# Feature moves in 2048-byte rows, and second-attention statistics one tile per step, in a four-stage gated transformer kernel

## The chip, the cores and the metric

One core of one Trainium2 chip runs the whole program. The metric is device time in microseconds (us) of one execution, less is better. TensorE (PE) multiplies, VectorE (DVE) and ScalarE (ACT) do element-wise work, GpSimd (POOL) does a few small operations, and SyncE (SP) issues most DMAs. Each engine runs its own instructions strictly in the order in which they stand; engines wait for each other by semaphores.

## The reference, cut to what matters

`x` is 8 sequences of 512 tokens with 512 features, in float32. Four stages follow each other, each with a layer norm in front and a gated residual behind.

```python
x = x + tanh(g_xattn[0]) * linear_attention(layernorm(x), ctx, Wq, Wg, bg, Wkv, Wo)   # "xa0"
x = x + tanh(g_ffn[0])   * gelu_ffn(layernorm(x), proj1, proj2)                       # "ff0", 2048 wide
x = x + tanh(g_xattn[1]) * softmax_attention(layernorm(x), ctx, mask)                 # "xa1", 64 context rows
x = x + tanh(g_ffn[1])   * grouped_experts(layernorm(x), router, gate_up, down)       # "ff1", 8 groups of 192
```

The second attention takes scores of the normed x against the 64 context rows, a softmax, and reads the context rows back. The last stage computes eight gated experts for every token (`silu(gate) * up`), weights them by a router that sees the normed x, and sums.

## The kernel before, in words

The batch is cut into 8 blocks of 512 tokens (4 tiles of 128). First the linear attention runs over all blocks, then the first feed-forward over all blocks (`ff0`, block b is called ff0_b), then second attention and experts together (`ff1_b`). Every large product uses a scheme with seven half-size products (m = 1 to 7) in place of eight. One such set of seven is a *unit*. A unit gathers its products in three PSUM banks x, w, z: x takes m = 1, 6, 7, 4 in this order, w takes 5 and 3, z takes 2. After m = 1, 6 and 7 ACT copies the bank x to SBUF (tiles u1, u6, u7, L922), and the next product may be added into that bank only after the copy: m = 6 waits for u1, m = 7 for u6, m = 4 for u7. An ff1 block has six such units in the order 1, 0, 3, 2, 5, 4, and then the down product (`SplitDown`, L1105), whose weights come as tiles of 256 KB from a ring of 16 buffers.

While PE works on one block, a generator (`prep_ff1(b)`) prepares the next one, one step after each product or after several. It has three parts. `normed(..., "xa1_b")` normalizes x for the second attention; `cross_attention` makes the scores (`pst`, L729), turns them (`psc`), takes exponentials (L753), turns back (`pe`), multiplies by the context (`pr`, L774) and adds to x (L776); `normed(..., "ff1_b")` normalizes the new x for the experts; then the router (`plt`, `pl`, `pw`) and the token sums `S` follow. `steps_of` spreads 34 steps over a block.

`normed` is the function that the change touches. DVE takes statistics of the four tiles (`st`, L487; `mv`, L488; `var`, L490; `nshift`, L494), POOL makes 1/sigma (L495, L497), ACT writes the four normed tiles `xn` (L507), DVE transposes them in 32x32 squares (L562), and 16 DMAs from SP's queue (L580), one for each pair of a 32-partition group and a group of feature columns, gather the squares into `xnT`, which has features on partitions. One such DMA moves 64 KB; before the change its rows are 512 bytes: four tiles, 32 partitions each.

Order: some engines run in the order written (`in_order`), the others in an order that a static scheduler works out when the kernel is built. In the last two stages only SP is held to program order, and from ff1 on none; `with here("vector")` holds single DVE instructions to it. The order on each engine is fixed before the run.

## Time and profile before

| what | value |
|---|---|
| median of 3 runs | 2036.1 us (2035.9 to 2041.35) |
| profiled execution, its own time | 2034.87 us |
| its span, first to last instruction | 2033.1 us |
| PE busy | 2003.0 us (99%) |
| DVE busy | 1512.3 us (74%) |
| ACT busy | 646.7 us (32%) |
| SP's DMA queue, share of 16 DMA engines | 73.6% |
| granted TensorE clock, mean | 0.999 |

The time of the profiled execution is what one run took; its span leaves out 1.8 us around it. The names in the trace carry neither block nor unit numbers (`x_ff`, `xnT_xa`), so a block is found by its time: the linear attention ends near 400 us, the ff0 blocks near 1140 us, and an ff1 block takes about 112 us. PE and PEld are the two halves of a product, its stream and its weight load, and two instructions stand for one float32 product.

### The profile page before, as it was taken

To read this page: it belongs to the slowest core of one execution; us is meant where nothing else is said; L and a number is where in the kernel's file an instruction comes from. 1 tells how busy PE (TensorE), PEld (TensorE's weight loads), DVE (VectorE), ACT (ScalarE), POOL (GpSimd) and SP (SyncE) were. 2 spreads that over 40 slices of the span, in tenths; PEclk is the share of its full clock that TensorE was granted. 3 is DMA by queue.
4 is the path that set the end of the run, shared out by engine and by line. 5 is a ranking of instruction groups with operands and counts; after the bars stand their busy time and mean duration, and the time that the engine had idled before them with its cause. 6 is when DMAs were issued, how large, how long until landed. Compare 5 with 4: busy or idle time off the path is not lost.

```text
span 2033.1 us, 34969 instructions
## 1 busy us (share of the span) xinstructions
PE 2003.0 (99%) x12428; PEld 1778.0 (87%) x12428; DVE 1512.3 (74%) x3012; ACT 646.7 (32%) x1294; POOL 95.9 (5%) x147
## 2 busy tenths in 40 slices
PE   9999999999999999999999999999999999999998
PEld 5888887889989899999988989898989888898988
DVE  4788888675857677777857787787778686876858
ACT  4533443323242424233233331313222232313122
POOL 3000000000000000000001010000001010100000
PEclk9999999999999999999999999999999999999999
DMA  7376556688979898989877869787878878786865
GB/s 211 127 217 189 178 156 175 231 304 276 341 236 347 264 341 260 314 291 297 305 245 233 294 217 294 230 291 212 294 238 266 262 234 273 215 288 211 277 203 172
DMA packets 357228, 508.79 MB, mean 250 GB/s; under 512 B 42944, under 2 KB 156768, under 8 KB 352960
## 3 DMA queue, kind: packets, MB, share of 16 engines
q1 hardware_dynamic: 349616, 479.79, 73.6%
q10 hardware_dynamic: 5856, 23.20, 3.1%
q0 software_dynamic: 1584, 3.57, 0.7%
q8 instruction: 100, 1.64, 0.3%
q14 instruction: 72, 0.59, 0.1%
HBM read 413.04 MB, written 69.27 MB: 237 GB/s over the span
## 4 chain that ended last, share of the span: by engine, by line
PE 47%; DVE 1%; DMA 1%; SPq 1%; ACT 0%; issue 0%; POOL 0%; DVEq 0%; POOLq 0%
PE x_ff L910 16%; PE w_ff L910 8%; PE x_ff_down L1105 7%; PE w_ff_down L1105 5%; PE z_ff L910 4%; PE z_ff_down L1105 2%; PE v_ff_down L1105 2%; PE pst L729 1%; PE pr L774 1%; SPq L580 0%; PE plt L789 0%; DMA w_ff<-ff_up 0%; DMA x_ff<-x_ff 0%; DVE xn_ff L562 0%; DVE st_xa L487 0%
## 5 line engine op out<-in xcount | busy, mean ns | idle before, releaser
L910 PE MATMUL w_ff<-S_ff,w_ff 128*128 128x256 f32 x1280 | 305.4, 380 | 2.7 <-DVE up_ff L1003 1.2
L910 PE MATMUL x_ff<-S_ff,w_ff 128*128 128x256 f32 x1280 | 304.0, 379 | 0.0
L910 PE MATMUL x_ff<-xnT_ff,w_ff 128*128 128x256 f32 x1280 | 299.1, 381 | 0.4 <-ACT u_ff L922 0.4
L922 ACT COPY u_ff<-x_ff 128x512 f32<-128x512 f32 x240 | 139.9, 583 | 463.4 <-PE x_ff L910 427.1
L910 PEld LDWEIGHTS w_ff<-S_ff,w_ff 128*128 128x128 f32 x1280 | 240.8, 190 | 39.5 <-DVE up_ff L1003 3.0
L910 PEld LDWEIGHTS x_ff<-S_ff,w_ff 128*128 128x128 f32 x1280 | 242.5, 190 | 34.2 <-ACT a_ff L60 0.8
L910 PEld LDWEIGHTS x_ff<-xnT_ff,w_ff 128*128 128x128 f32 x1280 | 240.4, 191 | 34.2 <-issue 1.8
L1105 PE MATMUL x_ff_down<-w_ff_down,split_ff_down 128*128 128x128 f32 x1344 | 161.8, 275 | 0.0
L1105 PEld LDWEIGHTS x_ff_down<-w_ff_down,split_ff_down 128*128 128x128 f32 x1344 | 155.8, 192 | 0.0
L910 PE MATMUL z_ff<-xnT_ff,w_ff 128*128 128x256 f32 x640 | 152.8, 380 | 0.0
L1119 DVE TENSOR_TENSOR part_ff_down<-part_ff_down 128x128 f32<-128x128 f32 x315 | 83.9, 285 | 73.2 <-ACT part_ff_down L1132 64.2
L910 PEld LDWEIGHTS z_ff<-xnT_ff,w_ff 128*128 128x128 f32 x640 | 119.9, 190 | 19.9 <-issue 4.5
L1105 PE MATMUL w_ff_down<-w_ff_down,split_ff_down 128*128 128x128 f32 x896 | 107.9, 275 | 0.0
L1105 PEld LDWEIGHTS w_ff_down<-w_ff_down,split_ff_down 128*128 128x128 f32 x896 | 103.9, 192 | 0.0
L970 ACT ACTIVATE a_ff<-a_ff,b_sb 128x256 f32<-128x256 f32 x128 | 58.1, 501 | 91.9 <-DVE a_ff L965 91.9
L1105 PE MATMUL w_ff_down<-w_ff_down,s_ff 128*128 128x128 f32 x672 | 83.1, 275 | 2.6 <-ACT part_ff_down L1132 2.6
L965 DVE TENSOR_TENSOR a_ff<-w_ff,u_ff 128x512 f32<-128x512 f32 x64 | 43.9, 685 | 53.8 <-ACT u_ff L922 53.2
L1105 PEld LDWEIGHTS w_ff_down<-w_ff_down,s_ff 128*128 128x128 f32 x672 | 80.1, 192 | 3.6 <-ACT part_ff_down L1132 2.8
L1003 DVE TENSOR_TENSOR up_ff<-w_ff,u_ff 128x512 f32<-128x512 f32 x96 | 65.6, 683 | 23.6 <-ACT u_ff L922 23.3
L1105 PE MATMUL x_ff_down<-w_ff_down,a_ff 128*128 128x128 f32 x672 | 82.8, 275 | 0.0
L1105 PEld LDWEIGHTS x_ff_down<-w_ff_down,a_ff 128*128 128x128 f32 x672 | 79.5, 192 | 0.4
L993 DVE SCALAR_TENSOR_TENSOR g_ff<-th_ff,x_ff 128x512 f32<-128x512 f32 x48 | 32.6, 680 | 63.2 <-ACT th_ff L992 63.2
(262 smaller groups left out, 3266.7 us busy)
## 6 DMA issues: line engine op xcount, KB each, us to landing
w_ff_down<-stream_ff SPq DMA_DIRECT2D x680, 256.0 KB
w_ff<-ff_up SPq DMA_DIRECT2D x560, 256.0 KB
stream_ff<-build_ff_down SPq DMA_DIRECT2D x49, 448.0 KB
x_ff<-x_ff SPq DMA_DIRECT2D x16, 1024.0 KB
share<-shares SPq DMA_DIRECT2D x64, 256.0 KB
xnT_ff<-xn_ff SPq DMA_DIRECT2D x240, 64.0 KB
ff_up<-build_ff_up SPq DMA_DIRECT2D x42, 256.0 KB
x_ff<-x_xa ACTq DMA_DIRECT2D x8, 1024.0 KB
```

The costliest lines, as they stand in the source:

```text
L729: nc.tensor.matmul(pst[ts(r, M), :], lhsT=ctxT[:, c, :], rhs=features_of("ff1", xnT)[:, c].rearrange("p (u r q) i -> p r u q i", u=2, r=2) ...
L774: nc.tensor.matmul(pr[t], lhsT=eT[half, t // 2, :], rhs=c2[half, :], start=True, stop=True)
L910: nc.tensor.matmul(p[:, n, :], lhsT=w[:, c, ts(n, P)], rhs=moving, **self.mark(m, 2 * n + c),)
L922: nc.scalar.copy(self.s[m], p)
L965: nc.vector.tensor_tensor(h, p, s, ALU.add)
L970: nc.scalar.activation(h[:, n, :], p[:, n, :], AF.Gelu, bias=b1_sb[:, f : f + 1])
L993: nc.vector.scalar_tensor_tensor(g, th, 1.0, p, ALU.add, ALU.mult)
L1003: nc.vector.tensor_tensor(u, p, s, ALU.add)
L1105: nc.tensor.matmul(p[bank][:, place, :], lhsT=operand[k][:, c, :], rhs=w[at // 4][:, ts(at % 4, P)], start=bank not in opened, stop=True, ...
L1119: return lambda: nc.vector.tensor_tensor(m(k), m(k), m(by), ALU.add)
```

## The change

Two parts, both in `normed`.

The tiles `xn` and `xnT` get another order of their free dimensions. `xn` was [tile, column group, 128], and is [column group, tile, 128]; `xnT` was [tile, q, 128], and is [q, tile, 128]. So the 16 gathering DMAs move 32 rows of 2048 bytes each in place of 128 rows of 512 bytes. All readers of `xnT` (token sums, `Up.product`, `pst`, `plt`) address it in the new order; `S` is laid out as (q, tile, column) outside the first attention.

The statistics of `xa1_b` keep DVE's program order, one tile per generator step (three more `yield`s). What comes behind them in `prep_ff1` so moves three steps back; `steps_of` stays 34.

```diff
-        xnT = work.tile([P, NC, S] if ph == "xa0" else [P, NT, NC, P], F32, tag="xnT", name=f"xnT_{tag}")
+        xnT = work.tile([P, NC, S] if ph == "xa0" else [P, NC, NT, P], F32, tag="xnT", name=f"xnT_{tag}")
...
-        with here(*(["vector"] if held or ph == "xa0" else [])):
+        with here(*(["vector"] if held or ph == "xa0" or tag.startswith("xa1") else [])):
             for t in range(NT):
                 st = small.tile([P, 6], F32, tag="st", name=f"st_{tag}_{t}")
                 nc.vector.bn_stats(st, xb[:, t, :])
                 nc.vector.bn_aggr(mv[:, t, :], st)
+                if tag.startswith("xa1") and t < NT - 1:
+                    in_order.discard("vector")
+                    yield
+                    in_order.add("vector")
...
-        xn = bank["xn"].tile([P, NT, D], F32, tag="xn", name=f"xn_{tag}")
+        xn = bank["xn"].tile([P, NC, NT, P], F32, tag="xn", name=f"xn_{tag}")
...
-                nc.vector.transpose(xn[:, at[t], :], xn[:, at[t], :])
+                nc.vector.transpose(xn[:, :, at[t], :], xn[:, :, at[t], :])
...
-                    nc.sync.dma_start(out=xnT[ts(l, HD), :, q, :], in_=xn[ts(q, HD), :, ts(l, P)])
+                    nc.sync.dma_start(out=xnT[ts(l, HD), q], in_=xn[ts(q, HD), l])
...
-        return xnT.rearrange("p t q (c i) -> p c (t q) i", c=NC)
+        return xnT.rearrange("p q t (c i) -> p c t q i", c=NC)
...
+            a11, a12, a21, a22 = (xnT[:, :, ts(r, 2), ts(h, 2 * HD)] for r in range(2) for h in range(2))
+            to = s.rearrange("p k c (q t i) -> p k (c q) t i", q=2, t=2)
...
-                        1: v[:, c, 0:8],
+                        1: v[:, c, 0:2],
```

The built programs have the same number of matmuls and of SP's DMAs in each kernel. Up to the last ff0 block (ff0_7) the two PE orders are the same; from there on the scheduler places the prepared work differently. In the ff1 blocks 1 to 6 of the changed kernel, for example, PE runs `pr`, then one matmul of m = 2 of the fourth unit (unit 2), then m = 6, 5, 7 of that unit, m = 1 of the next, and m = 4; ACT runs u6, th1, two of the four `xn` norms of `ff1_b`, u7, the other two norms.

More of the change, by code (lines that the diff above doesn't have):

```diff
@@ L528, in turn @@
                     nc.scalar.copy(
-                        xnT[:, t].rearrange("p q (c i) -> p c q i", c=NC),
+                        xnT[:, :, t].rearrange("p q (c i) -> p c q i", c=NC),
                         pt.rearrange("p c (q i) -> p c q i", q=NC),
@@ L568, in normed @@
                     t,
-                    xn[:, at[t], :].rearrange("p (l c e) -> p c l e", l=NC, c=NC),
+                    xn[:, :, at[t]].rearrange("p l (c e) -> p c l e", c=NC),
                     lambda of: of.rearrange("p (c l e) -> p c l e", l=NC, c=NC),
@@ L589, in features_of @@
         if ph == "xa0":
-            return xnT.rearrange("p c (g i) -> p c g i", i=HD)
-        return xnT.rearrange("p t q (c i) -> p c (t q) i", c=NC)
+            return xnT.rearrange("p c (t q i) -> p c t q i", q=NC, i=HD)
+        return xnT.rearrange("p q t (c i) -> p c t q i", c=NC)
     turned = [dram.tile([P, NC, M], F32, tag=f"turned{b}", name=f"turned_{b}") for b in range(B)]
@@ L681, in token_combinations @@
         s = work.tile([P, 4, 2, H2], F32, tag="S", name=f"S_{ph}_{b}", bufs=1)
-        v = features_of(ph, xnT)
-        a11, a12 = v[:, 0:2, 0:8], v[:, 2:4, 0:8]
-        a21, a22 = v[:, 0:2, 8:16], v[:, 2:4, 8:16]
-        to = s.rearrange("p k c (g i) -> p k c g i", i=HD)
+        if ph == "xa0":
+            v = features_of(ph, xnT).rearrange("p c t q i -> p c t (q i)")
+            a11, a12, a21, a22 = (v[:, ts(h, 2), ts(r, 2)] for r in range(2) for h in range(2))
+            to = s.rearrange("p k c (t i) -> p k c t i", t=2)
+        else:
+            a11, a12, a21, a22 = (xnT[:, :, ts(r, 2), ts(h, 2 * HD)] for r in range(2) for h in range(2))
+            to = s.rearrange("p k c (q t i) -> p k (c q) t i", q=2, t=2)
         nc.vector.tensor_tensor(to[:, 0], a21, a22, ALU.add)
@@ L689, in token_combinations @@
         nc.vector.tensor_tensor(to[:, 3], a12, to[:, 1], ALU.subtract)
-        return s
+        if ph == "xa0":
+            return to.rearrange("p k c t (q i) -> p k c t q i", i=HD)
+        return to.rearrange("p k q t (c i) -> p k c t q i", c=2)
     def prep_ff0(b):
@@ L731, in cross_attention @@
                     lhsT=ctxT[:, c, :],
-                    rhs=features_of("ff1", xnT)[:, c].rearrange("p (u r q) i -> p r u q i", u=2, r=2)[:, r],
+                    rhs=features_of("ff1", xnT)[:, c].rearrange("p (u r) q i -> p r u q i", r=2)[:, r],
                     start=c == 0,
@@ L791, in prep_ff1 @@
                     lhsT=router_sb[:, c, :],
-                    rhs=features_of("ff1", xnT)[:, c, ts(t, NC)],
+                    rhs=features_of("ff1", xnT)[:, c, t],
                     start=c == 0,
@@ L901, in product @@
                     moving = {
-                        1: v[:, c, 0:8],
-                        2: v[:, 2 + c, 0:8],
-                        4: v[:, 2 + c, 8:16],
-                        5: s[:, 0, c, :],
-                        6: s[:, 1, c, :],
-                        7: s[:, 2, c, :],
-                        3: s[:, 3, c, :],
+                        1: v[:, c, 0:2],
+                        2: v[:, 2 + c, 0:2],
+                        4: v[:, 2 + c, 2:4],
+                        5: s[:, 0, c],
+                        6: s[:, 1, c],
+                        7: s[:, 2, c],
+                        3: s[:, 3, c],
                     }[m]
```

## The prediction

> **What bounds the kernel now.** I read the page first: PE is busy 99% of the span, so a change is worth what it takes from, or adds to, PE's waits. Then the windows of 50 us, to see where PE waits; then the timeline there, for what each wait ends on; then PE's order in the two built programs.

> ```profile
> PE 2003.0 (99%) x12428; PEld 1778.0 (87%) x12428; DVE 1512.3 (74%) x3012; ACT 646.7 (32%) x1294; POOL 95.9 (5%) x147
> ...
> 1000.00:1050.00 50.00, 47.36 (x336) 44.74 (x335) 35.16 (x84) 14.72 (x29) 1.54 (x2) 1.00 0.85 279
> 1050.00:1100.00 50.00, 43.94 (x256) 35.41 (x255) 29.96 (x76) 24.19 (x53) 5.60 (x9) 0.97 0.71 228
> ...
> 1300.00:1350.00 50.00, 50.00 (x349) 45.84 (x348) 42.51 (x92) 14.06 (x29) 5.61 (x9) 1.00 0.82 264
> ```

> The first number after the stretch is its length, the next PE's busy time. The ff0 and ff1 blocks run without a wait, except where the first ff1 block is prepared (1000 to 1100). There:

> ```profile
> 1009.06 2.93 ACT L507 ACTIVATE xn_xa<-x_ff,nshift_xa,rstd_xa 128x512 f32<-128x512 f32 x4 [6.22 <-POOL nshift_xa L497]
> 1012.51 1.16 PE L1105 MATMUL w_ff_down<-w_ff_down,s_ff 128*128 128x128 f32 x8 [2.64 <-ACT part_ff_down L1132]
> 1062.20 1.99 PE L774 MATMUL pr<-ctxd,eT 64*128 64x512 f32 x8
> 1066.86 1.99 PE L910 MATMUL w_ff<-S_ff,w_ff 128*128 128x256 f32 x8 [1.18 <-DVE x_ff L776]
> 1070.84 2.93 ACT L507 ACTIVATE xn_ff<-x_ff,nshift_ff,rstd_ff 128x512 f32<-128x512 f32 x4 [0.87 <-POOL nshift_ff L497]
> 1074.54 11.56 SPq L60 DMA_DIRECT2D xnT_ff<-xn_ff  x16
> 1092.77 0.99 PE L1105 MATMUL v_ff_down<-w_ff_down,a_ff 128*128 128x128 f32 x6 [3.01 <-DMA w_ff_down<-stream_ff]
> 1093.55 3.54 PE L910 MATMUL x_ff<-xnT_ff,w_ff 128*128 128x256 f32 x8
> ```

> Four norms hold ACT for 2.93 us, PSUM copies stand behind them, PE waits 2.64 us. Later 16 moves hold SP for 11.56 us, weight tiles stand behind them, PE waits 3.01 us, and the next eight matmuls take 3.54 us where 1.89 is usual: the clock was halved.

> **What the change takes away.** *Moves.* One took 599 ns to issue (median), a weight tile, also in rows of 2048 bytes but with 128 of them, 320:

> ```profile
> L60 SPq DMA_DIRECT2D xnT_ff<-xn_ff x128: 585/599/1986, 408.7 to 1085.5; - x128
> L1493 SPq DMA_DIRECT2D w_ff_down<-stream_ff x296: 319/320/1732, 1188.8 to 2013.0; - x148
> ```

> The new move has 32 rows; between a quarter of 599 and 599 I take 320, so a batch takes 16 x 0.32 = 5.1 us, not 9.6 to 11.6. [...] I take the rows, but only the first block's batch is on PE's path. SP's new order also puts the two tiles for v_ff_down and the 1 MB x load ahead of it. Behind the batch stands tile 9: issued near pr + 17.5, needed near pr + 26.

> *First block.* In ACT's new order the norms of xa1_0 stand behind those copies (2.64 gone); their new place is ahead of u7 of ff0_7's first unit, due 11.7 us after the old block's last down product. Six small sums, two gated additions, two statistics and the copies before them put nshift at 5.9, the norms at 7.2 to 10.1, u7 at 10.7: 1.0 to spare, and a wait at that place if DVE is later than that. The accumulator lent to pr is next opened 6.9 us after pr, not 3.5, past DVE's 4.6 (1.18 gone). With the batch, the waits for plt (0.78), pl (0.38) and v_ff_down (3.01), the half clock (3.54 - 1.89 = 1.65) and 0.40 before pw go: 6.2. Together **10.0 us**.

> *Second block.* At 1188.61 and 1191.84 PE waits 0.43 and 1.24 for ACT and DVE, after DVE stood 2.79 us before a statistic whose x had not landed; program order places it later: **1.7**. Two waits for plt in later blocks: **1.2**. Sum **12.9 us**.

> **What costs nothing.** Transposes, norms and S take strided operands, as they do now: same element counts, 0.70, 0.73 and 0.68 us. Matmuls read runs of 32 elements from xnT already, 1.73 us for eight, as S contiguous. Were a strided matmul 1% slower, the page's 4480 of L910 in ff units at 0.216 us (1.73 / 8) would cost 10; nothing in the rows says so. POOL's xa1 pair moves behind the router products and three DMA issues; POOL is 5% busy. The xa1 moves go behind three to seven weight loads and x stores or shares; pst has slack of 8 us there. Shares go some eight tiles later, still a block's down product ahead.

> **What it adds.** Three steps later means other neighbours on ACT. Row, in the block at 1390:

> ```profile
> 1390.90 1.99 PE L774 MATMUL pr<-ctxd,eT 64*128 64x512 f32 x8
> ...
> 1393.42 0.74 DVE L776 SCALAR_TENSOR_TENSOR x_ff<-pr,coef,x_ff 128x512 f32<-128x512 f32 x1
> ...
> 1401.92 0.69 DVE L487 BATCH_NORM_STATS2 st_xa<-x_ff 128x6 f32<-128x512 f32 x1
> ...
> 1402.59 0.16 DVE L494 TENSOR_SCALAR nshift_ff<-mv_ff 128x4 f32<-128x4 f32 x1
> ...
> 1404.11 0.81 ACT L507 ACTIVATE xn_ff<-x_ff,nshift_ff,rstd_ff 128x512 f32<-128x512 f32 x1 [3.50 <-POOL nshift_ff L497]
> ```

> From pr to the first norm 13.21 us. Before, only u1 of a later unit stood behind it, with 1.3 us to spare (done 1405.4, wanted 1406.7). After, u7 of unit 2 stands behind two norms, and m = 4 waits for u7. In the new DVE order the first addition to x isn't late (pr + 1.16, as at 1063.36, not 2.52), two sums (1.20) and a st_xa (0.61) leave the stretch: 13.21 - 3.17 = 10.0. Two norms 1.43, u7 0.59: pr + 12.1. PE reaches m = 4 at 1.92 (pr) + 0.43 + 4 x 1.73 = 9.25. **A wait of 2.85 us**, in each of the six preparations of blocks 2 to 7. Low end: the first block's 8.64 (1062.20 to 1070.84), a wait of 1.4; high end: 13.21, a wait of 6.0. I take the row of the same kind of block less what left it.

> Two smaller ones, per block. At the start, three statistics (3 x 0.70) now stand ahead of DVE's up at 1373.00; the four xa1 norms then end near 1382.1, u6 of the second unit at 1382.65, wanted at 1382.25: 0.4 (0 to 2.5, if DVE is later). Between psc and pe 3.5 us are planned, th2 ahead of the exponentials makes it 3.7: 0.2 (0 to 1). Sum 6 x 3.45 = **20.7**.

> Preparing block 1, three norms stand before u7: 8.64 + three DVE operations 1.8 + 2.14 + 0.59 = 13.2 against 11.0: **2.2**. Block 0: four norms before u6 of the last ff0 unit, 8.64 + 2.86 + 0.59 = 12.1 against 10.6: 1.5, and 0.3 at pe: **1.8**.

> The new waits are near 3 us, so the clock must be asked. [...] Rows: a gap of 2.64 kept it, 3.01 behind thin work lost 1.65 us. [...] I take 0.

> **The sum.** -12.9 + 20.7 + 2.2 + 1.8 = +11.8. On the profiled execution's 2034.9: 2046.7; its time is 1.2 below the median of the runs shown, so I say **2047**.

> **Rivals.** *No wait at u7* (chance 0.16, not slower): if the chain from pr to the first norm takes under 7.2 us, u7 isn't held, and 12.9 less some 4 of small waits is left: 2025. It decides from 1.5 us of new wait per block downward: (12.9 - 4.0 of blocks 0 and 1) / 6. For it: the scheduler put the norms there, so by its own reckoning they are ready. Against: it did so at 1404 too, and u1, free to run from 1401.5, got ACT at 1404.83.
> *Low ends* (0.10): 1.4 per block and nothing else: 2034.9 - 12.9 + 8.4 + 4.0 = 2034, no change.
> *Clock as well* (0.09): half clock after every wait: 2047 + 10 = 2057.
> *The rows don't merge*: if a move still took 599 ns, SP would hold 9.6 us; in block 0 moves end at pr + 21.9, landed near 24, plt is due at 25: still hidden. It changes nothing; it is inside the other cases.
> The forecast has 0.65, its own range 2041 to 2060.

> **How the numbers follow.** 0.3%, 6 us, is about what can be told from no change. Slower 0.65 + 0.09 = 0.74, same 0.10, faster 0.16. The range from 2031 to 2062 leaves out the faster case and a few worse ones.

> **What would show it.** Moves at about 320 ns. No wait at the place of 1012 and of 1092, clock 1.00 there. In six blocks, 9 us after pr, a wait of m = 4 for ACT's u copy (L931) of 1.4 to 6 us: the group x_ff<-xnT_ff, 0.4 us of idle now, shows about 17 to 20. If that group still shows under 5, I am wrong.

## The result, and the profile after

The changed kernel takes 2054.3 us (median of 4 runs, 2050.95 to 2057.01) where the kernel before took 2036.0 beside it (4 runs). The ratio is 1.009, with a 95% interval of 1.0071 to 1.011: slower. The profiled execution took 2050.95 us, 16.1 more than that of before (2034.87), with a span of 2049.2.

From the page of the changed kernel, the engine row and the group that the prediction named (in that row: busy time, mean ns, then idle time ahead of the group and what ended it):

```profile
PE 2010.8 (98%) x12428; PEld 1779.0 (87%) x12428; DVE 1516.5 (74%) x3012; ACT 645.8 (32%) x1292; POOL 99.0 (5%) x147
...
L919 PE MATMUL x_ff<-xnT_ff,w_ff 128*128 128x256 f32 x1280 | 303.2, 383 | 15.1 <-ACT u_ff L931 14.5
```

The same group in the kernel before:

```profile
L910 PE MATMUL x_ff<-xnT_ff,w_ff 128*128 128x256 f32 x1280 | 299.1, 381 | 0.4 <-ACT u_ff L922 0.4
```

The group had 0.4 us of idle time, and has 15.1 (17 to 20 were forecast), nearly all ended by ACT's copy of u. The windows of the changed kernel, same columns as before, and under them the last one in the kernel before:

```profile
1000.00:1050.00 50.00, 50.00 (x354) 47.15 (x353) 38.70 (x90) 15.21 (x30) 1.23 (x2) 1.00 0.85 289
1050.00:1100.00 50.00, 48.75 (x323) 41.44 (x322) 36.95 (x85) 24.63 (x54) 1.88 (x3) 1.00 0.73 233
1250.00:1300.00 50.00, 47.11 (x222) 38.01 (x221) 38.34 (x72) 17.73 (x36) 2.87 (x4) 1.00 0.74 226
```

```profile
1250.00:1300.00 50.00, 50.00 (x252) 42.03 (x251) 39.20 (x74) 14.46 (x31) 1.23 (x2) 1.00 0.77 238
```

The first ff1 preparation (1000 to 1100) is nearly free of waits now, and a window with a later preparation, full before, lacks 2.9 us. The timeline there, around one `pr`:

```profile
1285.69 1.99 PE L783 MATMUL pr<-ctxd,eT 64*128 64x512 f32 x8
...
1288.25 2.05 DVE L785 SCALAR_TENSOR_TENSOR x_ff<-pr,coef,x_ff 128x512 f32<-128x512 f32 x3
...
1290.35 1.99 PE L919 MATMUL w_ff<-S_ff,w_ff 128*128 128x256 f32 x8 [0.32 <-DVE x_ff L785]
...
1293.91 1.89 PE L919 MATMUL x_ff<-xnT_ff,w_ff 128*128 128x256 f32 x8
...
1295.82 1.52 ACT L511 ACTIVATE xn_ff<-x_ff,nshift_ff,rstd_ff 128x512 f32<-128x512 f32 x2 [2.94 <-POOL nshift_ff L501]
1297.24 0.56 ACT L931 COPY u_ff<-x_ff 128x512 f32<-128x512 f32 x1
...
1297.85 1.99 PE L919 MATMUL x_ff<-xnT_ff,w_ff 128*128 128x256 f32 x8 [2.05 <-ACT u_ff L931]
```

Two norms hold ACT, u7 stands behind them, and m = 4 waits 2.05 us for it, in each of the blocks 2 to 7 (and 2.2 in block 1, behind three norms). The product that u7 copies (m = 7, issued at 1292.18) had ended by about 1294.1.

To compare sections I add up what PE loses: for two matmuls that follow each other, the time from start to start, less what the pair usually takes (216 ns after one of 256 columns, 112 after one of 128). For the few matmuls of other shapes one usual time, the median of both kernels, stands for both. It counts waits and half clock alike, also the small losses around `pst`, `pr` and `plt` that both kernels have (some 1.6 us a block). A block ends with its last down product.

| us lost on PE | before | after | difference |
|---|---|---|---|
| linear attention (to 400 us) | 32.6 | 32.9 | +0.2 |
| ff0 blocks, to 985 | 3.0 | 3.9 | +0.9 |
| preparation of ff1 block 0 | 13.2 | 4.4 | -8.8 |
| of block 1 | 4.1 | 3.9 | -0.2 |
| of blocks 2 to 7, together | 11.0 | 35.0 | +24.0 |
| sum | 64.0 | 80.0 | +16.1 |

The sum is the whole difference of the two profiled executions; what lies before the first matmul (1.1 us) and behind the last (6.0) is the same in both.

### The profile page after: what moved, and what is told of

Its sections match the earlier page's. It is cut to its first block, busy times and chain, and to the rows that moved or that the text cites. A ratio compares the mean times of both kernels' runs of the same rounds, so it can differ in the third digit from the quotient of the medians.

```text
span 2049.2 us, 34981 instructions
## 1 busy us (share of the span) xinstructions
PE 2010.8 (98%) x12428; PEld 1779.0 (87%) x12428; DVE 1516.5 (74%) x3012; ACT 645.8 (32%) x1292; POOL 99.0 (5%) x147
## 2 busy tenths in 40 slices
DMA packets 321902, 508.81 MB, mean 248 GB/s; under 512 B 42945, under 2 KB 109665, under 8 KB 317633
## 3 DMA queue, kind: packets, MB, share of 16 engines
q8 instruction: 101, 1.65, 0.3%
## 5 line engine op out<-in xcount | busy, mean ns | idle before, releaser
L919 PE MATMUL x_ff<-xnT_ff,w_ff 128*128 128x256 f32 x1280 | 303.2, 383 | 15.1 <-ACT u_ff L931 14.5
L931 ACT COPY u_ff<-x_ff 128x512 f32<-128x512 f32 x240 | 139.9, 583 | 466.8 <-PE x_ff L919 434.8
L919 PEld LDWEIGHTS x_ff<-xnT_ff,w_ff 128*128 128x128 f32 x1280 | 239.6, 191 | 53.7 <-ACT u_ff L931 18.8
```

Source lines behind the costliest of these rows:

```text
L919: nc.tensor.matmul(p[:, n, :], lhsT=w[:, c, ts(n, P)], rhs=moving, **self.mark(m, 2 * n + c),)
L931: nc.scalar.copy(self.s[m], p)
```

## The experiments

Ratios are to the kernel before, run on the same chip beside each; its median was 2034.0 us for the first eight kernels and 2033.0 for the last four. Several expectations below reckon in us from 2036, where the kernel before stood at the result; against those, compare the ratios.

### The two parts, each alone

`rows_alone` leaves the statistics as they were. Every engine then has exactly the order of before.

```diff
-        with here(*(["vector"] if held or ph == "xa0" or tag.startswith("xa1") else [])):
+        with here(*(["vector"] if held or ph == "xa0" else [])):
...
-                if tag.startswith("xa1") and t < NT - 1:
-                    in_order.discard("vector")
-                    yield
-                    in_order.add("vector")
```

> The rows of 2048 bytes alone, with the statistics as before. All engines keep the order of before. Theory: the changed kernel's trace shows moves of 588 ns where before had 599, so the rows are not where the time comes from or goes to: 2036 us, within 3, and the waits at the first ff1 block (some 10 us) all stay. Rival 1: a strided read of the matmuls, norms or sums costs: 4480 matmuls at 1% would give 2046. Rival 2: shorter transfers are worth the 6.2 us that my prediction gave the batch in the first block: 2030.

Measured: 2031.47 us, ratio 0.9986 (0.9978 to 0.9995). `stats_alone` is the opposite: the tiles' layout of before, with the statistics' part. Every engine has exactly the order of the changed kernel.

> The statistics' part alone, with moves in rows of 512 bytes as before. All engines have the order of the changed kernel. Theory: the whole change of time is here: 2054 us (2050 to 2058), a wait of 2.2 us for ACT's u copy in each preparation of blocks 1 to 7. Rival: part of the loss is the layout's, then 2036 to 2048.

Measured: 2051.12 us, ratio 1.0084 (1.007 to 1.0099). From its table of PE's waits (us in total, times, longest):

```profile
PE x_ff L914 <- ACT u_ff L926: 17.9, 14, 2.2
```

The changed kernel has the same row with the same 17.9. The loss is the statistics' part, and no cost of strided reads shows. The rows are worth a little, 0.14%, and not at the place that rival 2 named. In the first block of the kernel with rows alone:

```profile
PE v_ff_down L1110 <- DMA w_ff_down<-stream_ff: 2.8, 1, 2.8
```

v_ff_down still waits 2.8 us (3.0 before). In the two profiles, what went are the waits of later blocks for `plt` (1.4 us in two blocks), 1.3 us in block 1 and 1.2 us in the ff0 blocks. The last of these is of a kind that changes from run to run (see below), so the profiles show where the 0.14% can come from and not more.

### Where the copy stands among the norms

`u7_first` gives the norms of `ff1_b` one step more and holds them to program order on ACT alone, so that all four stand behind u7. On PE only the router's products (`plt`, `pl`, `pw`) and a few neighbours change places:

```diff
+        if tag.startswith("ff1") and b > 0:
+            yield
...
-            with here(*(["vector", "scalar"] if ahead else [])):
+            with here(*(["vector", "scalar"] if ahead else ["scalar"] if tag.startswith("ff1") and b > 0 else [])):
```

> The changed kernel, with the four norms of ff1 (blocks 1 to 7) one step later and in ACT's program order, so that u7 of unit 2 stands ahead of all four; PE's order is otherwise the same. Theory: the 7 waits of 2.2 us at m = 4 go, and the half clocks that follow some of them: 2054.3 - 15.5 - 3 to 7 = 2034 us (2031 to 2039), the waits of 0.7 and 0.5 us per block stay. Rival: the three steps themselves cost (what stands beside pr, pst and psc on PE), and u7 only shows it: another wait takes the place, 2048 or more.

Measured: 2030.02 us, ratio 0.9981 (0.9972 to 0.9989). From its timeline, the same place (the norms carry a helper's line, L60):

```profile
1288.84 3.62 PE L921 MATMUL x_ff<-xnT_ff,w_ff 128*128 128x256 f32 x16
1289.04 0.59 ACT L933 COPY u_ff<-x_ff 128x512 f32<-128x512 f32 x1 [1.24 <-PE x_ff L921]
...
1290.73 1.52 ACT L60 ACTIVATE xn_ff<-x_ff,nshift_ff,rstd_ff 128x512 f32<-128x512 f32 x2 [1.11 <-POOL nshift_ff L501]
```

u7 is copied at once, the sixteen matmuls of m = 1 and m = 4 run through, and the norms start 1.1 us later than the copy ends without anyone waiting for them. The losses of blocks 2 to 7 fall from 5.3 to 7.0 each to 3.0. Nothing took the place, and the rival fell.

`norms_one` and `norms_four` move the norms by one step without holding them (the same `yield` added, or one of those in `normed` removed), so that one or four of them stand ahead of u7.

> The changed kernel with one step more ahead of the norms of ff1 in blocks 1 to 7: in blocks 2 to 7 one norm instead of two stands ahead of u7 of unit 2 (block 1 keeps three). Theory: the wait of m = 4 is the place of u7 behind norms, each worth its 0.71 us: 2.05 - 0.71 = 1.34 us in each of the six, 4.3 us less in all and the half clocks with it: 2045 to 2049. Rival: the first norm comes later by the step as well, and the wait stays at 2.05: 2051 to 2054.

> The changed kernel with one step less ahead of the norms of ff1: all four norms stand ahead of u7 of unit 2, in all blocks from 1 to 7. Theory: the wait of m = 4 grows by two norms, to 2.05 + 1.42 = 3.47 us in blocks 2 to 7 (by one norm in block 1), 9.2 us more in all, 2063; with the clock halved after such a wait each time (1.7 us, as twice in the changed kernel's profile), up to 12 more: 2063 to 2072. Rival: the norms come earlier by the step as well, and the wait stays near 2: 2051 to 2056.

Measured: 1.0046 (1.0028 to 1.0064, 2042.51 us) and 1.0191 (1.0172 to 1.021, 2074.03 us). `norms_one` is `u7_first` without the hold, and PE's order is the same in both, instruction for instruction; only DVE's and ACT's differ, at the norms. So the 12 to 13 us between the two kernels are what the place of u7 among the norms is worth there, with one norm ahead in blocks 2 to 7 and three in block 1. The timeline with one norm ahead:

```profile
1294.05 0.81 ACT L513 ACTIVATE xn_ff<-x_ff,nshift_ff,rstd_ff 128x512 f32<-128x512 f32 x1 [2.93 <-DMA share<-shares]
1294.77 0.56 ACT L933 COPY u_ff<-x_ff 128x512 f32<-128x512 f32 x1
...
1295.39 1.99 PE L921 MATMUL x_ff<-xnT_ff,w_ff 128*128 128x256 f32 x8 [1.34 <-ACT u_ff L933]
```

and with four:

```profile
1301.29 1.89 PE L917 MATMUL z_ff<-xnT_ff,w_ff 128*128 128x256 f32 x8
...
1301.46 2.93 ACT L509 ACTIVATE xn_ff<-x_ff,nshift_ff,rstd_ff 128x512 f32<-128x512 f32 x4 [2.93 <-POOL nshift_ff L501]
...
1304.91 1.99 PE L917 MATMUL x_ff<-xnT_ff,w_ff 128*128 128x256 f32 x8 [1.73 <-ACT u_ff L929]
```

With one norm the wait is 1.34, as expected to the hundredth. With four, the scheduler put another product (m = 2 of the next unit, 1.73 us) ahead of m = 4; 1.73 of it and 1.73 of wait make 3.46, where 3.47 was expected. The step does not move the norms' start: in all three kernels the first norm starts 1.9 us after m = 1 of the next unit (1295.82 against 1293.91 in the changed kernel). No half clock follows this wait of 1.73 (the eight matmuls behind it take 1.99 us), though I had allowed for one each time. The kernel with four is still slower than expected because new waits come behind it: 1.9 us at the start of the down product in six blocks, and 3.0 for `pw` in the first block; their causes stay open. The granted clock of that profiled execution is 0.996, of before 0.999.

### Where else the change costs

`adds_in_order` is u7 first, with the four additions of `pr` to x held in DVE's program order:

```diff
+        with here("vector"):
             for t in (3, 0, 1, 2):
                 nc.vector.scalar_tensor_tensor(xb[:, t, :], pr[t], coef[:, t : t + 1], xb[:, t, :], ALU.mult, ALU.add)
```

> The kernel with u7 first, and the four additions of pr to x in VectorE's program order, so that the first statistic no longer stands between the first addition and the other three. Theory: w_ff waits 0.48 us in each of blocks 2 to 7 for the last of these additions, because of that statistic (0.61 us); it goes, six times: 2.9 us less than u7 first, ratio to before 0.9967. Rival: the additions of pr[0] and pr[1] come later in the new order and another accumulator waits for them: no change, 0.998.

Measured: 2028.79 us, 0.9977 (0.9966 to 0.9987). The loss of blocks 2 to 7 falls from 3.0 to 2.5 each, so the 0.48 us goes: the accumulator lent to `pr` is freed by the addition of t = 3, which the program has first and the scheduler had put last. But the first block loses 6.5 instead of 4.3, and most of the gain is given back. `adds_from_2` holds the additions only from block 2 on.

> u7 first, with the additions of pr in program order from block 2 on only. In the run with them in order everywhere the blocks 2 to 7 lost 2.5 us each instead of 3.0, but the first block lost 6.5 instead of 4.3. Theory: the two are independent: 58.1 - 6 x 0.5 = 55.1 us of losses, ratio to before 0.9966, 2027 us where before has 2034. Rival: 0.9977 to 0.9981, no better than the two it is made from.

Measured: 2027.95 us, 0.9968 (0.9956 to 0.9981). The sections behave as said (2.5 a block), the first block loses 5.3; the intervals of the two overlap, so that it is better is likely and not shown.

### The three steps and the program order, each alone

`order_no_steps` is the changed kernel without the three `yield`s, `steps_no_order` with them and without `here("vector")`.

> The changed kernel without the three steps between the statistics; they stay in VectorE's program order. On ACT all four norms stand ahead of u6 of unit 2 in blocks 1 to 7. Theory: not the three steps as such, but a copy behind norms is what costs, and it costs here too: some 2 us per block as in block 1 of the run with the first block alone, ratio 1.003 to 1.009. Rival: the three steps are the cause: without them the kernel is no slower than with rows alone, 0.9986.

> The changed kernel with the three steps, but without VectorE's program order for the statistics. On ACT all four norms stand ahead of u6 of unit 2 from block 2 on, and two ahead of u7 in block 1. Theory: as for program order alone, 1.003 to 1.009. Rival: program order is the cause: 0.9986.

Measured: 1.0225 (1.0209 to 1.0241, 2079.63 us) and 1.0033 (1.0022 to 1.0043, 2039.55 us). The largest waits of PE, first with order alone, then with steps alone:

```profile
PE x_ff L915 <- ACT u_ff L927: 19.6, 7, 3.2
PE w_ff L915 <- DVE up_ff L1008: 8.1, 6, 1.3
```

```profile
PE w_ff L917 <- DVE up_ff L1010: 10.4, 10, 2.1
PE w_ff_down L1112 <- ACT part_ff_down L1139: 2.6, 1, 2.6
```

Neither half is free, and neither is the cause by itself. With order alone u6 stands behind four norms, 3.2 us in each of the blocks 2 to 7 instead of the 2 that I expected, and the granted clock of the profiled execution is 0.991, where before has 0.999. With steps alone I had the sum right and the place wrong: only one copy behind norms is waited for (2.3 us in block 1), the rest are waits for DVE's `up`, which stands behind transposes and statistics that the scheduler was free to put there. Its second line is the wait of before at 1012: it is the program order that moved the norms of xa1_0 out of the way of the part copies, and with order alone that wait is gone. The other large wait of the first block goes by the steps: v_ff_down still waits 3.1 us with order alone, and not at all with steps alone.

### How a move's issue is paid

`split_moves` is rows alone, with each move issued as two.

```diff
-                    nc.sync.dma_start(out=xnT[ts(l, HD), q], in_=xn[ts(q, HD), l])
+                    for h in range(2):
+                        nc.sync.dma_start(out=xnT[ts(l, HD), q, ts(h, 2)], in_=xn[ts(q, HD), l, ts(h, 2)])
```

> Rows alone, and each move issued as two of 32 rows of 1024 bytes. Theory (issue is a fixed cost of such a move, whatever its rows): about 588 ns each still, a batch of 32 takes 18.8 us, and the first ff1 preparation loses up to 9 us more for v_ff_down: 2036 to 2041. Rival (issue goes with bytes, or with how fast earlier moves drain): 300 ns each, a batch of 9.5 us, time as with rows alone, 2031.

Measured: 2221.16 us, 1.0912 (1.0888 to 1.0936). The moves as SP issues them (ns, shortest, median, longest), and PE's waits:

```profile
L60 SPq DMA_DIRECT2D xnT_ff<-xn_ff x256: 507/588/1402, 410.6 to 1174.0; - x128
```

```profile
PE plt L795 <- DMA xnT_ff<-xn_ff: 47.9, 8, 12.7
PE x_ff_down L1111 <- DMA w_ff_down<-stream_ff: 28.0, 8, 5.7
PE pst L735 <- DMA xnT_xa<-xn_xa: 20.5, 7, 4.5
PE v_ff_down L1111 <- DMA w_ff_down<-stream_ff: 15.9, 8, 4.2
```

The theory of the issue holds: half the bytes, the same 588 ns. Its sum was far too low, since I counted the first batch only. There are 23 batches (368 moves in 16s), each holds SP some 9 us longer (16 more issues of 588 ns), and scores, router and weights wait in nearly every block. The moves are hidden before, with little to spare. The kernel is not the same but for the issues: the scheduler also placed DVE's work differently from 535 us on, and ACT's and PE's later. The four DMA waits shown, 112 us, are most of the 188 us lost, so the direction is safe; how the rest divides is not shown.

### A version that beats both

`first_only` has the rows, and the statistics' part for `xa1_0` alone (`tag == "xa1_0"` in place of `tag.startswith("xa1")`).

> Rows of 2048 bytes, and the statistics' part for the first block only (xa1_0). Theory: the gain of the first preparation (2.6 us before 1022, 6.1 us after it, by PE's losses in the two traces) and the loss of blocks 2 to 7 (23 us) are independent, so this keeps the gain and drops the loss: 2036 - 8.7 = 2027 us (2024 to 2031). Rival: what the first block gains is paid back in block 1, whose preparation then meets another order: 2033 or more.

Measured: 2029.93 us, 0.998 (0.997 to 0.9989). The first block keeps its gain (4.6 us lost), and blocks 2 to 7 lose 1.5 to 1.8, as with rows alone; but block 1 loses 10.0 (rows alone: 2.7). My theory of independence fell (by ratio it expected 0.9956), and the rival was right. Its timeline in block 1:

```profile
1174.16 2.93 ACT L511 ACTIVATE xn_ff<-x_ff,nshift_ff,rstd_ff 128x512 f32<-128x512 f32 x4 [4.96 <-DMA x_ff<-x_ff]
...
1177.00 0.56 ACT L931 COPY u_ff<-x_ff 128x512 f32<-128x512 f32 x1
...
1177.61 3.15 PE L919 MATMUL x_ff<-S_ff,w_ff 128*128 128x256 f32 x8 [2.14 <-ACT u_ff L931]
```

Again a copy behind norms, four this time, and eight matmuls in 3.15 us where 1.89 is usual. `first_u7` cures just that:

```diff
+        if tag == "ff1_1":
+            for _ in range(4):
+                yield
...
-            with here(*(["vector", "scalar"] if ahead else [])):
+            with here(*(["vector", "scalar"] if ahead else ["scalar"] if tag == "ff1_1" else [])):
```

> The statistics' part for the first block only, and in block 1 alone the norms of ff1 held four steps later in ACT's program order, behind u6 and u7 of unit 2. Theory: the first block's gain was paid back in block 1 by the copy behind four norms (2.3 us) and a half clock behind it (1.65): both go, ratio 0.998 - 4/2034 = 0.996. Rival: block 1's preparation ends four steps later and its router (1.2 to 2.4 us in that run) waits that much longer: 0.998 or more.

Measured: 2022.16 us, 0.995 (0.9936 to 0.9963): half a per cent faster than before. Block 1 loses 2.2 us, not 10.0; the waits for the router went as well, so the rival fell. The same two windows as above, of this kernel:

```profile
1050.00:1100.00 50.00, 48.27 (x333) 41.32 (x332) 39.89 (x97) 25.01 (x53) 4.95 (x8) 1.00 0.75 245
...
1250.00:1300.00 50.00, 49.86 (x238) 41.30 (x238) 38.23 (x75) 15.71 (x33) 2.43 (x4) 1.00 0.71 216
```

## Why the prediction was right, and where it was not

It said slower, 2047 us in a range of 2031 to 2062. The measured median is 7 us above, the profiled execution 4.3 above its own sum of 2046.7. Place and mechanism were right; several sizes were not, and some of their errors cancel.

**The wait for u7**, the step that carries the sum, was right in place and kind, and is shown by the series over the norms ahead of u7: none, 0; one, 1.34; two, 2.05; four, 1.73 behind a product of 1.73. From `pr` to the first norm I had 10.0 us, and it took 10.13; u7 was to be done at `pr` + 12.1, and was (1297.80). The wait was sized 2.85 and PE lost 2.21 there, because PE came to m = 4 later than I had it: 0.48 us are lost on the way at w_ff. (The terms of PE's way add up to 9.27, not 9.25, and those of the rival without a wait to 2026, not 2025; nothing hangs on either.)

**The lent accumulator** was the step that failed in sign. I said that the next use of the bank comes after DVE's additions (1.18 us gone). It does not: in blocks 2 to 7, where before had no such wait, 0.48 us each are lost for the addition that frees the bank, and in the first block 0.69 of the 1.18 stay. I had reckoned when the additions begin, not that the one for the lent bank comes last and behind a statistic.

**u6 behind the xa1 norms** at the start of a block: 0.4 predicted, 0.68 lost. **The gap at `pe`**: 0.2 predicted, nothing lost. Together 2.21 + 0.48 + 0.68 = 3.37 a block, where I had 3.45. That this comes so close is luck: the wait for u7 is 0.64 smaller than forecast, and the 0.48 that I had at nothing and the larger wait for u6 make up for it.

**The clock.** I took 0 for waits near 2.85 us. No run shows that 0, nor the 10 us of the rival that gave a half clock to every wait: in the profiled execution two of the seven waits of 2.05 to 2.2 us are followed by one, 1.7 us each, 3.4 in all. The rival was right in two cases of seven.

**The moves.** I took the duration of a weight tile, 320 ns. That was wrong. From the changed kernel's table of SP's issues:

```profile
L60 SPq DMA_DIRECT2D xnT_ff<-xn_ff x128: 507/588/1397, 409.2 to 1087.7; - x128
...
L584 SPq DMA_DIRECT2D xnT_ff<-xn_ff x112: 507/588/1152, 1184.1 to 1890.3; - x112
```

The rows did merge: the page counts 321902 packets, before 357228, a fall of 35326, some 96 for each of 368 moves. The issue fell from 599 to 588 ns. The nearest row was not the nearest: the weight tile shared the 2048 bytes, but comes from DRAM to 128 partitions.

**The first block** came out nearly right for another reason. I had 10.0 off and 1.8 on, 8.2 net. Measured are 9.3 off (2.64, 0.49 of the 1.18, and the 6.2) and 0.5 on: 8.8. The 0.5 is at u6 of the last ff0 unit, which stands behind four norms as forecast, with 1.5. The batch of moves took 10.3 us, not 5.1 (and with rows alone 11.4, where before had 11.6):

```profile
1071.56 0.80 SPq L60 DMA_DIRECT2D w_ff_down<-stream_ff  x2
1078.00 10.30 SPq L60 DMA_DIRECT2D xnT_ff<-xn_ff  x16
1088.35 11.34 SPq L60 DMA_DIRECT2D w_ff_down<-stream_ff  x18
...
1089.02 1.95 PE L1114 MATMUL v_ff_down<-w_ff_down,a_ff 128*128 128x128 f32 x16
```

v_ff_down does not wait all the same, because SP's new order has its two tiles ahead of the batch (1071.56). So of my two reasons for the 3.0 us the order was the one that held, the shorter batch was not, and with it went the half clock and the waits for `plt`, `pl` and `pw`. The statistics alone, with moves as before, bring the first block to 4.2. The wait of 2.64 at the old place of 1012 is gone, and the norms of xa1_0 cost nothing at their new place. So the first block's size is right and one of its reasons wrong; that part is luck too.

**Block 1** was to be 0.5 worse and is 0.2 better: the wait behind three norms came as forecast, 2.2, but 2.4 went and not 1.7. **The later waits for `plt`**, 1.2, went; rows alone, with the statistics as before, lacks them too.

The sum by what was measured: -8.8 - 0.2 + 24.0 is +15.0, where I had +11.8; the half clocks are 3.4 of it. Another 0.9 is in the ff0 blocks, where only the moves' rows differ: one wait of 2.2 us for weights with a half clock behind it, where before has two waits, 3.1 together. Such waits, the longest of 1.1 to 2.6 us, stand in the ff0 blocks of every profile here (`split_moves` left aside) and change from run to run; the prediction was wrong to call these blocks free of waits.

## What to carry to other kernels

Work that is moved by a few steps gets new neighbours on each in-order engine: for every instruction that PE waits for, list what now stands ahead of it and when that is ready; here one copy of 0.6 us behind two norms of 0.7 cost more than all that the change repaired. A cure for a stall that happens once should be given to that one place, and the next block looked at too, since its preparation meets the moved order. The issue of a small transfer is priced by a row of the same kind, same memories and same partitions, and not by one with the same row length: here 588 ns, where the move of before had 599 and the weight tile 320.

## What the runs showed of the hardware

**The clock was halved behind two of seven waits of 2.05 to 2.2 us.** In the changed kernel, after two waits of the same length:

```profile
1528.31 3.14 PE L919 MATMUL x_ff<-xnT_ff,w_ff 128*128 128x256 f32 x8 [2.05 <-ACT u_ff L931]
1531.24 2.48 PE L919 MATMUL w_ff<-S_ff,w_ff 128*128 128x256 f32 x8
...
1645.23 1.99 PE L919 MATMUL x_ff<-xnT_ff,w_ff 128*128 128x256 f32 x8 [2.05 <-ACT u_ff L931]
1647.06 1.89 PE L919 MATMUL w_ff<-S_ff,w_ff 128*128 128x256 f32 x8
```

The first eight take 3.14 us after one wait, 1.99 after the other. The granted clock behind the first of them (last but two of these numbers) is below 1.00:

```profile
1530.00:1534.00 4.00, 4.00 (x15) 3.33 (x14) 2.05 (x4) 0.75 (x2) 0.00 (x0) 0.70 0.32 93
```

**The issue of a move within SBUF to 32 partitions took a median of 588 to 599 ns**: 599 with 128 rows of 512 bytes, 588 with 32 of 2048 and with 32 of 1024 (`split_moves`). A weight tile of 128 rows from DRAM took 320. Whether the memories or the 32 partitions set it stays open; fewer moves of more partitions were not tried.
